# Cross attention of a decoder layer: seven block products for eight in the second element's queries and scores and in both elements' attended values

## The chip, the cores and the metric

The kernel runs on one core of a Trainium2 chip. A core has a matrix engine (TensorE, PE in the profile, whose weight loads are shown apart as PEld), three engines for elementwise work (VectorE or DVE, ScalarE or ACT, GpSimd or POOL), an engine that here only issues transfers (SyncE or SP), and 16 DMA engines. Each engine takes its instructions in the order written; semaphores make one wait for another. The on-chip memory SBUF has 128 partitions; TensorE writes to PSUM, a small memory of eight banks.

The metric is the time of one execution in microseconds (us), as the device measures it; lower is better. Several executions of the kernel before gave a median of 1125.8 us (1124.88 to 1126.19).

## The reference, cut to what matters

A decoder layer in float32 on x of shape (2, 512, 512): self attention with 16 heads, cross attention to a context of 1024 rows per element, a feed-forward part (FFN), each followed by a residual sum and a layernorm.

```python
x = layernorm(x + self_attention(x, ...))        # 16 heads of 128, weights as 4-bit codes times scales

Q = x @ W_qkv[:512].T                            # (2, 512, 512)
scores = coef * einsum('bsd,bnd->bsn', Q, ctx)   # (2, 512, 1024)
scores = scores - max(scores)
thr = top_k(scores, 54)[0][..., -1:]             # 54 are kept in each row
scores = where(scores < thr, -inf, scores)
x = layernorm(x + einsum('bsn,bnd->bsd', softmax(scores), ctx) @ W_o.T)

gate, up = split(x @ w_gate_up.T, 2)             # 2048 each
x = layernorm(x + (silu(gate) * up) @ w_down.T)
```

The cross attention is the part in question: a 512x512x512 product for the queries of each element, 512x512x1024 for the scores, 512x1024x512 for the attended values, and 512x512x512 for the projection behind them.

## The kernel before, in words

The 128 partitions hold the contracted dimension of every product. P is 128, KD = 4 pieces of 128 make the model dimension, NT = 4 tiles of 128 rows an element, NK = 8 pieces the 1024 context rows. HK = 2 and HS = HD = 256 are halves.

**Seven for eight.** `seven` (before, it serves the self attention's projections, `gu` of the FFN's first product and `pd` of its second) multiplies matrices cut into 2x2 blocks with seven block products in place of eight. It needs sums of blocks beforehand: four for the stationary side (`combine_a`) and four for the moving side (`combine_b`); `ALEFT` and `BRIGHT` map blocks and sums to the product numbers. One call makes two 128-row pieces of the output, 512 columns each, by products of 128x256. Products 1, 6 and 7 go to the bank `r`; after each, ScalarE keeps a copy in a buffer `u` (`keep`, L161 to L162). Products 2, 5, 4 and 3 go to the double bank `z`. VectorE then adds `z` and `u`: `on_second` for the second output half, `on_first` for the first. Product 3 is put off (`rest`) and issued inside the next call by `close`, so that TensorE does not wait for ScalarE.

**Cross attention.** It does not use `seven`. `xquery` (L346) makes Q with TensorE, 512 columns wide, and ScalarE copies each bank. `xscores` (L373) makes one tile of 128 rows by 1024 scores, which ScalarE evicts scaled by `coef` (L386). `clip` (L389) finds the 54th-largest score of each row on VectorE: MAX8 gives the eight largest, MATCH_REPLACE8 strikes them out, seven times; ScalarE then takes exponentials, VectorE masks and sums, and ScalarE scales. `xattend` (L448) multiplies the weights with the context and projects the result with `xpo` (L474), added to the residual. For element 0 the weights are transposed by TensorE (`transpose_weights`, L432); for element 1 `turn_weights` (L418) has VectorE transpose blocks of 32 and SP move them with 16 transfers a group (`turn`, L244). The queries' input x1T of element 1 and x2T of both are turned in the same way, which leaves rows in an order by blocks of 32; `in_order` and `turned` name the two orders.

**Order of the work.** It is written out by hand: engines run their parts in the order in which the program issues them, subject to a scheduler that moves independent instructions. The buffers are places in SBUF with a tag each (`place`), one tensor at a time; the tag decides when the next tensor may be written. Element 0's search runs beside the self attention; its attended values lie around `project(last)`, the last projection of the self attention (`ro` and `zo`). Then follow `xpo` of element 0, `xq` and `xs` of element 1, `up(0, 0)` and `down(0, 0)`, the first half of the FFN of element 0 (L861, L922), while element 1's search (`search1`) is advanced two steps with every block of `up`, then `up(0, 1)`, `xattend` of element 1, `down(0, 1)` and the FFN of element 1. In `up`, a block loads `wgu` (512 KB), GpSimd makes four sums (`wc`), and `seven` gives two results: VectorE's `ut` (L897) and `gt` (L903), which ScalarE turns into `sg` and VectorE multiplies into `h` (L906). Sums of `h`, `hc`, follow (L879 to L883). `combine_wdn` makes the second product's weight sums `dc` on GpSimd.

## Time and profile before

| | us |
|---|---|
| median of the runs | 1125.8 (1124.88 to 1126.19) |
| the profiled execution | 1123.9 |
| its span, first to last instruction | 1122.1 |
| TensorE busy | 1091.8 (97% of the span) |
| VectorE busy | 609.2 (54%) |
| GpSimd busy | 504.9 (45%) |
| ScalarE busy | 414.2 (37%) |
| xq of element 1, in the chain | 13.86 |
| xpo of element 0, in the chain | 13.73 |

An instruction line of the profile has the source line, engine, operation, output<-inputs by the program's names, the shape as partitions x elements, a count, busy time in us, mean ns of one, and behind the bar the engine's idle time just before, with what ended it. The chain of waits is followed back from the last instruction: at each piece to what released it, or to the one before on its engine. Matmuls overlap, and each float32 matmul has two records, so that the mean of one record is longer than the share of it that counts. The granted clock of TensorE was 0.998 of full speed.

### The profile page before, as it was taken

How to read it: one execution, taken by the hardware profiler on the slowest of the kernel's cores; microseconds unless marked ns; L12 is line 12 of the kernel's file. 1: busy time of each engine (PE TensorE's matmuls, PEld its weight loads, DVE VectorE, ACT ScalarE, POOL GpSimd, SP SyncE). 2: the span in 40 equal slices, each digit the busy share in tenths (PEclk: the TensorE clock that was granted, in tenths of full speed). 3: DMA queues.
4: the chain of work that ended last, by engine and by line, in shares of the span. 5: the costliest groups of instructions: out<-in, count | busy, mean ns of one | idle time of the engine just before them, and what ended most of it. 6: DMA issues, size and time to landing. Idle time of an engine off the chain costs nothing.

```text
span 1122.1 us, 12521 instructions
## 1 busy us (share of the span) xinstructions
PE 1091.8 (97%) x4144; PEld 775.2 (69%) x4144; DVE 609.2 (54%) x983; ACT 414.2 (37%) x927; POOL 504.9 (45%) x498
## 2 busy tenths in 40 slices
PE   7999999999999999999999999999999999999997
PEld 5666776677677667574657666446878886888886
DVE  5645445345444446278997543249995423543353
ACT  2453445335443534434445542123433212221221
POOL 4844725845945644523372430130445530464730
PEclk9999999999999999999999999999999999999999
DMA  9435545554554465433325446420214300520300
GB/s 353 125 101 173 171 122 205 181 174 136 181 191 110 135 219 163 144 100 107 103 92 181 112 109 232 129 56 19 95 38 161 121 20 19 169 85 29 133 18 37
DMA packets 66607, 141.63 MB, mean 126 GB/s; under 512 B 12656, under 2 KB 14704, under 8 KB 66544
## 3 DMA queue, kind: packets, MB, share of 16 engines
q1 hardware_dynamic: 66400, 140.32, 39.3%
q8 instruction: 33, 0.54, 0.2%
q10 hardware_dynamic: 144, 0.52, 0.1%
q14 instruction: 30, 0.25, 0.1%
HBM read 99.90 MB, written 2.10 MB: 91 GB/s over the span
## 4 chain that ended last, share of the span: by engine, by line
PE 74%; DVE 14%; ACT 5%; POOL 2%; DMA 2%; issue 1%; SPq 1%; DVEq 0%; ACTq 0%; POOLq 0%
PE sc L600 8%; PE av L643 8%; PE zqk L152 8%; PE zgu L152 6%; PE rqk L152 6%; PE xav L459 5%; PE rgu L152 5%; PE zo L152 4%; PE zv L152 4%; PE zpd L152 4%; DVE work L398 4%; PE ro L152 3%; DVE top L401 3%; PE rv L152 3%; PE rpd L152 3%; PE xq L351 2%
## 5 line engine op out<-in xcount | busy, mean ns | idle before, releaser
L643 PE MATMUL av<-pt,v 128*128 128x512 f32 x256 | 121.6, 592 | 0.0
L607 DVE TENSOR_REDUCE nm<-sc 128x2 f32<-128x1024 f32 x64 | 78.2, 1222 | 74.5 <-PE sc L600 74.5
L600 PE MATMUL sc<-k,q 128*128 128x512 f32 x256 | 117.3, 599 | 0.7 <-DVE q L586 0.5
L99 POOL TENSOR_TENSOR wc<-wqk 128x256 f32<-128x256 f32 x31 | 24.9, 803 | 191.6 <-PE zqk L152 179.2
L623 DVE STREAM_TRANSPOSE tq<-p 128x512 f32<-128x512 f32 x128 | 85.3, 699 | 34.8 <-ACT p L620 27.5
L620 ACT ACTIVATE p<-p,sm 128x512 f32<-128x512 f32 x128 | 86.2, 723 | 4.9 <-DVE sm L619 4.9
L600 PEld LDWEIGHTS sc<-k,q 128*128 128x128 f32 x256 | 47.3, 190 | 58.9 <-issue 51.2
L611 ACT ACTIVATE p<-sc,nm 128x512 f32<-128x512 f32 x128 | 86.9, 686 | 1.6 <-ACT nm L608 0.2
L522 POOL TENSOR_TENSOR wqk<-wqk,sqk 128x512 f32<-128x512 f32 x52 | 65.9, 1288 | 40.4 <-DMA wqk<-in_wqk 25.5
L162 ACT ACTIVATE ugu<-rgu 128x256 f32<-128x256 f32 x96 | 36.2, 378 | 101.8 <-PE rgu L152 101.8
L99 POOL TENSOR_TENSOR wc<-wgu 128x256 f32<-128x256 f32 x32 | 28.9, 902 | 95.0 <-PE zgu L152 67.0
L643 PEld LDWEIGHTS av<-pt,v 128*128 128x128 f32 x256 | 48.5, 190 | 31.0 <-issue 27.3
L162 ACT ACTIVATE uqk<-rqk,bqkv_sb 128x256 f32<-128x256 f32 x96 | 45.2, 474 | 66.5 <-PE rqk L152 65.3
L152 PE MATMUL rqk<-x0c,wc 128*128 128x256 f32 x256 | 67.3, 385 | 1.0 <-ACT uqk L162 0.6
L152 PE MATMUL rgu<-x2c,wc 128*128 128x256 f32 x256 | 66.2, 381 | 0.7 <-POOL wc L100 0.4
L152 PEld LDWEIGHTS rqk<-x0c,wc 128*128 128x128 f32 x256 | 46.9, 190 | 21.3 <-ACT uqk L162 10.7
L379 PE MATMUL xs<-memT,qt 128*128 128x512 f32 x128 | 57.9, 600 | 1.6 <-ACT p L611 1.3
L934 POOL TENSOR_TENSOR res<-res,upd 128x512 f32<-128x512 f32 x12 | 15.6, 1296 | 96.7 <-DVE res L933 96.7
L401 DVE MAX8 top<-work 128x8 f32<-128x1024 f32 x48 | 58.5, 1219 | 0.8
L459 PE MATMUL xav<-at,mem 128*128 128x256 f32 (+1 forms) x192 | 55.9, 450 | 0.0
L152 PEld LDWEIGHTS rgu<-x2c,wc 128*128 128x128 f32 x256 | 48.1, 190 | 8.9 <-POOL wc L100 1.6
L661 ACT ACTIVATE ot<-av,bqkv_sb 128x512 f32<-128x512 f32 x28 | 19.2, 687 | 85.9 <-PE av L643 85.9
(203 smaller groups left out, 2309.4 us busy)
## 6 DMA issues: line engine op xcount, KB each, us to landing
pt<-tq SPq DMA_DIRECT2D x512, 64.0 KB, 2.0
wgu<-in_wgu SPq DMA_DIRECT2D x32, 512.0 KB, 3.3
wqk<-in_wqk SPq DMA_DIRECT2D x28, 512.0 KB, 4.9
sqk<-in_wqk_s SPq DMA_DIRECT2D x27, 512.0 KB, 3.8
wdn<-in_wdn SPq DMA_DIRECT2D x4, 2048.0 KB, 8.3
wv<-in_wv SPq DMA_DIRECT2D x7, 1024.0 KB, 5.3
sv<-in_wv_s SPq DMA_DIRECT2D x14, 512.0 KB, 6.1
wo<-in_wo SPq DMA_DIRECT2D x7, 1024.0 KB, 5.3
```

Source lines behind the costliest of these rows:

```text
L152: nc.tensor.matmul(o, left[k][:, cols], right[k], start=start and k == 0, stop=k == len(left) - 1, skip_group_check=not start,)
L162: nc.scalar.activation(u[:, i, :], r, AF.Identity, bias=at)
L379: nc.tensor.matmul(sc[:, cols], qts[b][:, k, t * P : (t + 1) * P], memTs[b][k][:, cols], start=(k == 0), stop=(k == KD - 1),)
L401: nc.vector.max(top, work)
L459: nc.tensor.matmul(av[:, h * n : (h + 1) * n], mems[b][k][:, m * P : (m + 1) * P], ats[b][h][k], start=(k == 0), stop=(k == NK - 1),)
L522: eng.tensor_tensor(part[:, w], part[:, w], sct[:, w], ALU.mult)
L600: nc.tensor.matmul(scs[:, n, :], q[:, (t + n) * P : (t + n + 1) * P], k, start=True, stop=True,)
L607: nc.vector.reduce_max(nms, scs, axis=AX.X, negate=True)
L611: nc.scalar.activation(pr, scs[:, t % 2, :], AF.Exp, bias=nms[:, t % 2 : t % 2 + 1], scale=HSCALE, accum_out=sm,)
L620: nc.scalar.activation(pr, pr, AF.Copy, scale=sm)
L623: nc.vector.transpose(tq[:, :, :, t, :].rearrange("p n k c -> p k n c"), pr.rearrange("p (k n a) -> p k n a", n=NB, a=BLK),)
L643: nc.tensor.matmul(av, vs[u // GH][:, k, j * P : (j + 1) * P], pt[:, :, k, :], start=(k == 0), stop=(k == NT - 1),)
```

## The change

- `xquery` of element 1 is replaced by `seven_xquery`: `coef` is multiplied into wq by ScalarE, GpSimd makes the four sums of wq, `combine_turned` makes the sums of x1T on VectorE, and the results are added by VectorE (`put`) in place of ScalarE's copies. VectorE also makes the sums of the queries (`sums_a`) for the next step.
- `xscores` of element 1 is replaced by `seven_xscores`: four calls of `seven`, with sums of the context (`combine_memT`) made on GpSimd. A call gives two score tiles (s and 2 + s) half of their columns, added by VectorE. ScalarE's evictions go.
- `xattend` uses `seven` for both elements: sums of the context (`combine_mem`) on GpSimd, sums of the attention weights on VectorE (`combine_at` for element 0, inside `turn_weights` for element 1). The projection adds its four pieces in the order 0, 2, 3, 1.
- `seven` gets an option `late` that issues product 2 ahead of product 1.
- `combine_wdn(0, 0)` moves behind the scores. The second search takes the tiles in the order 0, 2, 1, 3 and has one work buffer in place of two. `up(0, ...)` has three buffers for `wgu` in place of four.

The queries and scores of element 0 stay as they are. The core of the diff:

```diff
+    def sums_a(eng, a, c, steps):
+        for n, w in enumerate(steps):
+            a00, a01, a10, a11 = (f[:, w] for f in a)
+            eng.tensor_tensor(c[0][n], a10, a11, ALU.add)
+            eng.tensor_tensor(c[1][n], c[0][n], a00, ALU.subtract)
+            yield
+            eng.tensor_tensor(a10, a00, a10, ALU.subtract)
+            eng.tensor_tensor(c[2][n], a01, c[1][n], ALU.subtract)
+            yield
+
+    def sums_b(eng, b, c):
+        b00, b01, b10, b11 = b
+        eng.tensor_tensor(c[0], b01, b00, ALU.subtract)
+        eng.tensor_tensor(c[1], b11, c[0], ALU.subtract)
+        eng.tensor_tensor(b01, b11, b01, ALU.subtract)
+        eng.tensor_tensor(c[2], b10, c[1], ALU.subtract)
+        return BRIGHT(b, (c[0], c[1], b01, c[2]))
...
+        if late:
+            product(2, z[:, 1, :])
         product(1, r)
         keep(0, bias[0])
-        product(2, z[:, 1, :])
+        if not late:
+            product(2, z[:, 1, :])
...
+    def put(dst, z, u, is_turned=True):
+        if not is_turned:
+            nc.vector.tensor_add(dst.rearrange("p (h s) -> p h s", h=2), z, u)
+            return
+        o = in_order(dst)
+        for h in range(2):
+            nc.vector.tensor_add(
+                o[:, 2 * h : 2 * h + 2],
+                *(f[:, h, :].rearrange("p (i t c) -> p i t c", t=NT, i=NB // 2) for f in (z, u)),
+            )
+
+    def seven_xquery(b, w_tag, q_tag, c_tags):
+        w = xw["wq"]
+        for k in range(KD):
+            nc.scalar.activation(w[:, k, :], w[:, k, :], AF.Copy, scale=coef)
+        wc = combine_a(nc.gpsimd, blocks_t(w), place(w_tag, (4, HK, HD), f"wqc{b}"))
+        qt = place(q_tag, (KD, S), f"qt{b}")
+        q4 = blocks_t(qt)
+        c12 = place(c_tags[0], (2, HK, HS), f"qc{b}_12")
+        c4 = place(c_tags[1], (HK, HS), f"qc{b}_4")
+        for m in range(HK):
+            def second(z, u, m=m):
+                put(qt[:, HK + m, :], z, u)
+            def first(z, u, m=m):
+                put(qt[:, m, :], z, u)
+                c = [c12[:, 0, m : m + 1]], [c12[:, 1, m : m + 1]], [c4[:, m : m + 1]]
+                for _ in sums_a(nc.vector, q4, c, [slice(m, m + 1)]):
+                    pass
+            seven(f"xq{b}_{m}", wc, xcs[b], slice(m * P, (m + 1) * P), second, first)
+        close()
+        qts[b] = ALEFT(q4, (c12[:, 0], c12[:, 1], q4[2], c4))
+
+    def combine_memT(b, tags):
+        mts = []
+        t4 = place(tags[2], (2, HK, HS), f"mT{b}_4")
+        for n in range(2):
+            g = slice(n * S, (n + 1) * S)
+            b4 = [f[:, :, g][:, :, h] for f in memTs[b] for h in (slice(0, HS), slice(HS, S))]
+            t12 = place(tags[n], (2, HK, HS), f"mT{b}_{n}")
+            mts.append(sums_b(nc.gpsimd, b4, (t12[:, 0], t12[:, 1], t4[:, n])))
+        memTs[b] = mts
+
+    def seven_xscores(b):
+        for s in range(NT // 2):
+            for n in range(2):
+                def add(z, u, s=s, n=n, h=1):
+                    o = sts[b, 2 * h + s][:, n * S : (n + 1) * S]
+                    put(o, z, u, False)
+                seven(
+                    f"xs{b}_{s}_{n}",
+                    qts[b],
+                    memTs[b][n],
+                    slice(s * P, (s + 1) * P),
+                    add,
+                    lambda z, u, add=add: add(z, u, h=0),
+                    late=s == 0 and n == 0,
+                )
+        close()
...
     def clips(b, tags):
-        for t in range(NT):
-            yield from clip(b, t, tags[t % len(tags)])
+        for n, t in enumerate(range(NT) if b == 0 else (0, 2, 1, 3)):
+            yield from clip(b, t, tags[n % len(tags)])
...
-        yield from turn([sts[b, t] for t in range(NT)], NK, list(shaped), dests)
+        b4, c = ats[b], []
+        for t, _ in enumerate(turn([sts[b, t] for t in range(NT)], NK, list(shaped), dests)):
+            yield
+            if t == 1:
+                two = place(c_tags[0], (2, NK // 2, NT * 2, BLK), f"atc{b}")
+                c = [two[:, 0], two[:, 1], place(c_tags[1], (NK // 2, NT * 2, BLK), f"atc{b}_4")]
+            for g in (0, 1) if t == 1 else (t,) if t > 1 else ():
+                sums_b(nc.vector, *([f[:, :, g::NT, :] for f in fs] for fs in (b4, c)))
+        ats[b] = BRIGHT(b4, (c[0], c[1], b4[1], c[2]))
...
+    def combine_mem(b, tags):
+        hk = NK // 2
+        a4 = [f[:, :, h] for f in mems[b] for h in (slice(0, HD), slice(HD, D))]
+        a4 = a4[0], a4[2], a4[1], a4[3]
...
+        steps = [slice(k, k + 2) for k in range(0, hk, 2)]
+        mems[b] = ALEFT(a4, (c1, c2, a4[2], [c[:, k] for c in c4 for k in range(hk // 2)]))
+        yield from sums_a(
+            nc.gpsimd, a4, ([c1[:, w] for w in steps], [c2[:, w] for w in steps], c4), steps
+        )
+
+    def combine_at(b, tags):
+        c = [place(tag, (NK // 2, HS), f"atc{b}_{n}") for n, tag in enumerate(tags)]
+        ats[b] = sums_b(nc.vector, ats[b], c)
...
     def xattend(b, ot_tags):
+        oth = [place(tag, (2, S), f"xo{b}_{n}") for n, tag in enumerate(ot_tags)]
+        ot = [t[:, n, :] for t in oth for n in range(2)]
+        for m in range(HK):
+            seven(
+                f"xav{b}_{m}",
+                mems[b],
+                ats[b],
+                slice(m * P, (m + 1) * P),
+                lambda z, u, m=m: put(ot[HK + m], z, u, b == 1),
+                lambda z, u, m=m: put(ot[m], z, u, b == 1),
+            )
             yield
+        close()
         for t in range(NT):
             po = bank("r", f"xpo{b}_{t}")
-            for k in range(KD):
+            for k in (0, 2, 3, 1):
...
+            free_sc = [f"sc{(scale_count[0] + n) % 3}" for n in range(3)]
+            for _ in combine_mem(0, ("wqk2", *free_sc[:2])):
+                pass
             transpose_weights(0, ("xT1", "xc1"))
     load_memT(1)
+    combine_at(0, (free_sc[2], "work", "ot0"))
...
     turn_x(1, "v0", "v1", "x1T")
+    combine_turned(nc.vector, 1, "v0", "x1")
...
+    combine_memT(1, ("wqk3", "wqk4", "ot1"))
...
-            wt = place(("sc0", "sc1", "wqk1", "wqk2")[n % 4], (KD, 2, P), f"wgu{i}_{b}")
+            wt = place(("sc0", "sc1", "wqk1", "wqk2")[n % (3 + b)], (KD, 2, P), f"wgu{i}_{b}")
...
     load_wdn(0, 0)
-    for _ in combine_wdn(0, 0):
-        pass
     layernorm(0, "b")
     turn_x(0, "xc0", "xT0", "x2T")
     combine_turned(nc.vector, 0, "xc0", "x2")
-    xquery(1)
+    seven_xquery(1, "xT1", "xc1", ("sc1", "p3"))
     score_tiles(1, (("v0", 2), ("v1", 2)))
-    for t in range(NT):
-        xscores(1, t)
-    search1 = clips(1, ("sc2", "work"))
-    hc = up(0, 0, nc.vector, search1)
+    seven_xscores(1)
+    for _ in combine_wdn(0, 0):
+        pass
+    search1 = clips(1, ("work",))
+    hc = up(0, 0, nc.vector, search1, combine_mem(1, ("wqk2", "sc2", "p2", "p3")))
     down(0, 0, hc)
     load_wdn(0, 1)
-    search1 = chain(search1, turn_weights(1, ("ot0", "ot1", "ot0", "ot1"), ("cmb0", "cmb1")))
+    search1 = chain(search1, turn_weights(1, ("ot0", "ot1", "ot0", "ot1"), ("cmb0", "cmb1"), ("v0", "work")))
```

## The prediction, made before the changed kernel ran

> **What bounds the kernel now.** I read the page's busy times and slices first, then the chain of waits, the groups and stretches of the middle of the kernel, and last the timeline of TensorE where it idles.
>
> ```profile
> span 1122.1 us, 12521 instructions
> PE 1091.8 (97%) x4144; PEld 775.2 (69%) x4144; DVE 609.2 (54%) x983; ACT 414.2 (37%) x927; POOL 504.9 (45%) x498
> PE   7999999999999999999999999999999999999997
> DVE  5645445345444446278997543249995423543353
> PE 74%; DVE 14%; ACT 5%; POOL 2%; DMA 2%; issue 1%; SPq 1%; DVEq 0%; ACTq 0%; POOLq 0%
> ```
>
> TensorE is busy in 97% of the span at full granted clock, and is 74% of the chain. So products taken from it shorten the kernel, unless somebody else is late there. VectorE's slices show the two places where that can be: two runs of 9s, the searches for the 54th-largest score; the later one lies from 757 to 841 us. The chain shows the stages to be changed:
>
> ```profile
> 698.09 18.88 PE xav L459 x44
> 716.97 13.73 PE xpo L474 x32
> 730.70 13.86 PE xq L351 x32
> 744.57 7.93 PE xs L379 x18
> 753.24 1.24 DVE top L392
> 797.61 0.68 DVE ut L897
> ```
>
> From 698 to 752 TensorE works without a break. From 753 the chain runs over VectorE's search, and between 797 and 830 it runs on VectorE almost throughout. What the engines do there, by stretch (from and to, then busy us and count of PE, PEld, DVE, ACT, POOL, then clock, DMA share, GB/s):
>
> ```profile
> 700.00:720.00 20.00, 20.00 (x48) 8.93 (x47) 4.18 (x11) 4.87 (x8) 0.00 (x0) 1.00 0.42 119
> 740.00:760.00 20.00, 20.00 (x47) 8.57 (x46) 9.18 (x14) 3.67 (x6) 0.00 (x0) 1.00 0.19 46
> 760.00:780.00 20.00, 19.75 (x61) 11.14 (x60) 19.66 (x26) 7.90 (x12) 0.00 (x0) 1.00 0.08 27
> 800.00:820.00 20.00, 20.00 (x94) 17.39 (x93) 19.97 (x33) 5.47 (x13) 8.16 (x10) 1.00 0.24 79
> 820.00:840.00 20.00, 18.40 (x83) 15.14 (x82) 19.83 (x31) 7.94 (x11) 10.15 (x12) 1.00 0.08 27
> ```
>
> Before 760 VectorE and GpSimd have room. From 760 to 840 VectorE is full, and TensorE loses its first microseconds to it:
>
> ```profile
> 830.51 0.70 PE L152 MATMUL zpd<-wdn,h 128*128 128x256 f32 x2 [0.78 <-DVE h L906]
> 864.49 1.10 PE L152 MATMUL zgu<-x2T,wc 128*128 128x256 f32 x4 [1.31 <-DVE ut L897]
> ```
>
> **What is removed.** The products' price comes from these groups (each matmul has two records) and the chain:
>
> ```profile
> L351 PE MATMUL xq<-x1T,wq 128*128 128x512 f32 x64 | 28.1, 594 | 0.0
> L459 PE MATMUL xav<-at,mem 128*128 128x512 f32 x64 | 28.0, 592 | 0.0
> L459 PE MATMUL xav<-at,mem 128*128 128x256 f32 x128 | 28.0, 379 | 0.0
> L379 PE MATMUL xs<-memT,qt 128*128 128x512 f32 x128 | 57.9, 600 | 1.6 <-ACT p L611 1.3 <-ACT s L386 0.3
> ```
>
> The xpo piece of the chain has 32 records in 13.73 us, 0.429 us each; a 128x256 record takes half, and eight of them 1.73 us. So xq of the second element is 13.7 us, xs of it 27.5 us, xav of each element 27.5 us. One eighth of each goes: 1.72 + 3.44 + 3.44 + 3.44 = **12.0 us**. That is the ceiling: nothing else leaves TensorE.
>
> **What is added, stage by stage.**
>
> *Sums of mem for element 0* (8 GpSimd additions of 128x512, 1.27 us each by the oc and vc groups, 10.2 us) are queued before the last wo blocks' dequantisation. GpSimd is busy 9.43 of 20 us from 620 to 640 and 7.43 from 640 to 660; the last output block needs its combined weights over 25 us later. I take 0. Without that cover each late microsecond would be one of TensorE's, 10.2 at most.
>
> *Sums of the attention weights of element 0* (4 VectorE operations of 128x1024, about 1.2 us each by the MAX8 row of that width) follow the eight ScalarE copies. TensorE still has about 5 us of other products and the first two of xattend, which need no sum. 0; up to 3 if GpSimd's sums of memT meet VectorE's operations.
>
> *project(last), layernorm, the way to x1T.* The attended products of element 0 leave less filler, so the last projection ends about 4.7 us later (702.6 for 697.9). The 16 transfers of x1T, now issued from 705.5 to 714.9 with 2.0 us to landing, then land by 722; the four new sums of x1T (0.69 us each, as the x2 ones) are done by 725. TensorE wants x1T at 727.1 (730.7 less 3.44) and its sums two products, 1.7 us, later. 0, with 4 to 5 us to spare.
>
> *Sums of memT (8), of mem (8, two of them left for the search) and of wq (4)* for element 1 are 18 GpSimd additions here, 22.9 us. GpSimd is empty from 680 to 720, and the wq sums, queued last, wait for xT1, which xattend(0) frees; they end near 720 against 727. 0.
> The wdn sums, moved behind the scores, then fill 720 to 736. The first wgu load of up(0,0) that has to wait for qc1's buffer gets it near 761, is combined by 768 and wanted at 770.7: 0, but tight.
>
> *xq to xs.* Before, ScalarE copies of qt followed each bank. Now the last product must be kept, added by two put operations and summed by three of the 128x256 additions on VectorE (0.41 us each where alone) ahead of the products of xs that use sums; "late" puts another product first to cover part. I take **0.5 us**, between 0 and 1.5.
>
> *xs to the search.* This is where the gain is given back. TensorE reaches up(0,0) 8.6 us earlier (1.72 + 3.44 + 3.44), but a score tile is complete only after its second half's seventh product and two additions: I place the first MAX8 at 756.2, 3 us later than now. From there, by the changed kernel's order of instructions, VectorE has to do 17 MAX8 and 15 MATCH_REPLACE8 before the last h of this half (1.25 to 1.275 us with their loads: 40.8), two s operations 2.6, one transpose 1.2, 24 operations ut, gt and h at 0.61 start to start (14.6), sums of h 4.4, four puts 2.5, small ones 0.6: 66.7 us. The same pricing on the 23 and 19 of the kernel before, with its share of the rest, gives 78.5, where the trace has 77.2 (753.24 to 830.46). So the last h comes at 821.8 to 823 instead of 830.5, while TensorE wants it at 819.7. TensorE's idle time in this half goes from 1.85 to about 3.1: **+1.3 us**.
>
> *The rest of the search* moves into down(0,0) and the first blocks of up(0,1). ut of the third such block is done about 41 us after that h, and TensorE wants it at 38.3. With one work buffer, each tile's exponentials on ScalarE keep VectorE waiting up to 1 us before the next tile. I expect 3.4 us of idle time in place of 1.31 + 0.41: **+1.7 us**.
>
> *Attention weights of element 1*: 16 additions of 128x256 on VectorE between the turning transfers. The last transfer lands near 886 (SP issues them in order, among wgu loads), its sums end at 888, TensorE wants them at 890.5. 0, and 2 us to spare. xpo's order of k hides the last two puts. ScalarE gets lighter, because eviction of 16 score banks (0.69 us each) becomes three keeps of 128x256 per seven. The second half of the FFN of element 0 from the second down on, and all of element 1's, is as before. For the tight hand-overs together (sums of at, wgu, turned weights) I add **0.5 us**.
>
> [...] The row first: an addition of h (hc, L882) takes 0.41 us alone and 0.95 beside GpSimd's 1.70 us one, so a meeting costs about 0.5 us on VectorE and as much on GpSimd. Of the 28 added GpSimd operations few meet two-input VectorE work, since VectorE is busy only 13.4 of the 40 us after 680; six meetings would be 3 us, off the path.
> [...]
>
> **The sum.** -12.0 + 0.5 + 1.3 + 1.7 + 0.5 = -8.0 us. The profiled execution took 1123.9 (span 1122.1, 1.8 around it), 1.9 below the median 1125.8 of the runs. It would become 1115.9 (span 1114.1), the median **1117.8**.
>
> **Rivals.**
> 1. *VectorE absorbs it.* If the search starts with the second half's add at about 753 as now, and transfers keep their room, only 0 to 1.5 us come back: 1113.8 to 1115.3. For it: the pricing above came out 1.3 us too long on the kernel before.
> 2. *VectorE becomes the bound* from the first score to the third block of up(0,1). If the put operations and sums collide with GpSimd and the last h moves only to 827 to 829, the extra stall there is 5 to 7 us instead of 1.3, and with 1.7 more later 1121 to 1123.5. For it: VectorE is at 19.8 of 20 us for 80 us. Against it: six MAX8 and four MATCH_REPLACE8 fewer stand before that h.
> 3. *Slower: the gate weights with three buffers for four.* A buffer is freed by its unit's last product and wanted combined two units later, 2 x 14 x 0.432 = 12.1 us. Load (3.3) and four sums (0.73 each, 2.9) need 6.2. If SP's order (16 turning transfers are 10 us of issue) makes every load over 6 us late, each unit waits; the gain is gone from 1.0 us a unit in eight units, and from 1.3 (10.3 us in all) the kernel is slower. At 1.5: -8 + 12 = +4, 1129.8. Against it: only the turning stretches put such a queue on SP.
> 4. *The change doesn't do what it says*: if the seven products ran at more than 1.73 us per eight records, no gain. The gu products have this form already, at 385 ns against 379 for xav.
>
> **How the numbers follow.** My forecast's own case (1115.3 to 1120.5) has 0.55, rival 1 0.13, rival 2 0.20; 0.06 lies between it and no gain, rival 3 has 0.06. Differences under 0.2% (2.3 us) can't be told from no change here. Faster than 1123.5 are the first three, 0.88; same 0.06, slower 0.06. The range 1114.0 to 1123.0 leaves out about 0.16.
>
> **What would show it.** Right: xav, xq and xs as 128x256 products, 24.1, 12.0 and 24.1 us for an element; xq starting near 727, up(0,0) near 763; first MAX8 of the second search near 756; VectorE full until about 862; TensorE's idle time ahead of zpd and zgu ended by VectorE's h and ut, 3 to 4 us more in all; GpSimd busy near 540. Wrong: idle time of TensorE ended by GpSimd's wc or by wgu's transfers in every unit, by x1T before xq, or by the turned weights before xav of the second element.

## The result, and the profile after

The changed kernel took 1119.8 us (median of seven executions, 1117.0 to 1122.7), the kernel before 1125.2 beside it: ratio 0.9948, 95% interval 0.9932 to 0.9965. Run again on another chip it had 0.9954 (0.9939 to 0.9969). It is faster by half a per cent, 5 to 6 us where 8.0 were forecast; the forecast range, 1114.0 to 1123.0, holds it.

The page of the profiled execution (1119.8 us) has these lines in place of those of before: span, busy times, the slices of TensorE and VectorE, and the chain of waits by engine.

```profile
span 1118.0 us, 12865 instructions
PE 1083.0 (97%) x4248; PEld 798.0 (71%) x4248; DVE 641.1 (57%) x1043; ACT 415.3 (37%) x941; POOL 540.3 (48%) x526
PE   7999999999999999999999999989999899999997
DVE  5544445435345436268997554468999733543353
PE 72%; DVE 15%; ACT 6%; DMA 2%; POOL 2%; issue 1%; DVEq 0%; ACTq 0%; POOLq 0%; SPq 0%
```

TensorE's row has 8s now where it had only 9s: in the slices from 727 to 755 and from 866 to 894 us. The matmul groups say that the change does what it says. Of xq, xav and xs, 64 + 64 + 128 records of 128x512 fell to 32 + 0 + 64, and 128 records of 128x256 (xav) to none. Counted in units of 128x256 that is 448 fewer, and 392 new ones came. 56 x 0.216 = 12.1 us of products are gone. What came in their place is in TensorE's timeline (start, us, instruction, then the idle time before it and what ended it):

```profile
714.07 2.00 PE L174 MATMUL rxav<-at,mem 128*128 128x256 f32 x8 [0.48 <-ACT uxav L184]
716.54 1.13 PE L590 MATMUL xpo<-wo,xo 128*128 128x512 f32 x2 [0.47 <-ACT uxav L184]
737.73 1.13 PE L174 MATMUL rxq<-x1c,wqc 128*128 128x256 f32 x4 [0.95 <-ACT uxq L184]
746.63 1.13 PE L174 MATMUL zxq<-x1T,wqc 128*128 128x256 f32 x4 [2.15 <-DVE qt L396]
749.56 0.70 PE L174 MATMUL zxs<-mT,qc 128*128 128x256 f32 x2 [0.26 <-DVE qc L134]
823.41 0.70 PE L174 MATMUL zpd<-wdn,h 128*128 128x256 f32 x2 [0.43 <-DVE h L1028]
871.12 1.13 PE L174 MATMUL zgu<-x2T,wc 128*128 128x256 f32 x4 [3.09 <-DVE ut L1019]
```

With 0.45 and 0.38 near 660 and 672, 0.20 and 0.23, TensorE's idle time in the changed part is 9.1 us; the same list of before adds up to 3.85. So 5.2 of the 12.1 us went to new waits. Another 1.0 was lost before the change begins: a product that started at 633.78 starts at 634.74, and from 35 to 40 us this execution has a granted clock of 0.66 where the profile before has 1.00 (the last section comes back to it). That leaves 1.8 to the measured 4.1 of the spans. Between that product and the zpd product near 960 us TensorE's busy time fell by 10.5 us, not by 12.1. Each restart costs a little (the first four records after a wait take 1.10 to 1.13 us, not 1.03), but there are only four waits more than before, some 0.4 us by an estimate of 0.1 each; the rest I can't place.

Two waits are the big ones: 2.15 at the hand-over from queries to scores, 3.09 in the second half of the FFN of element 0. VectorE's timeline ahead of the first shows its queue at work, not idle:

```profile
742.28 1.03 DVE L134 TENSOR_TENSOR qc<-qt 128x256 f32<-128x256 f32 x1
743.35 0.83 DVE L135 TENSOR_TENSOR qc<-qc,qt 128x256 f32<-128x256 f32 x1
744.11 0.94 DVE L137 TENSOR_TENSOR qt<-qt 128x256 f32<-128x256 f32 x1
744.97 0.94 DVE L138 TENSOR_TENSOR qc<-qt,qc 128x256 f32<-128x256 f32 x1
745.83 0.74 DVE L396 TENSOR_TENSOR qt<-zxq,uxq 128x256 f32<-128x256 f32 x2
```

The put that TensorE waits for is the last line. Ahead of it in VectorE's queue are the four sums of the first piece, at 0.83 to 1.03 us where 0.42 is the time alone (in the run without the down weights' sums, below). On GpSimd the sums of the down weights, which were to be done by 736, last until 743, and the gate weights' sums queued behind them fill the microseconds of the queries' sums:

```profile
733.17 1.26 POOL L976 TENSOR_TENSOR dc<-wdn 128x512 f32<-128x512 f32 x1 [11.01 <-DVE mvb L321]
741.77 1.27 POOL L980 TENSOR_TENSOR dc<-wdn,dc 128x512 f32<-128x512 f32 x1
742.99 0.91 POOL L99 TENSOR_TENSOR wc<-wgu 128x256 f32<-128x256 f32 x1
745.59 0.90 POOL L99 TENSOR_TENSOR wc<-wgu 128x256 f32<-128x256 f32 x1
```

The down weights' sums began at 725.3 before, at 733.2 now. SP issues the load of wdn at 724.64 instead of 717.00, with 8.4 us to landing. (VectorE is named as the releaser at 733, but the load landed at that moment.) The load does not wait for its place, which holds the context of element 0: the last product that reads this context ends at 716.1. It stands in SP's queue behind the 16 transfers of x1T. SP's timeline before:

```profile
705.49 10.01 SPq L257 DMA_DIRECT2D x1T<-x1Tt  x16
717.00 0.37 SPq L840 DMA_DIRECT2D wdn<-in_wdn  x1
```

and after:

```profile
714.52 10.02 SPq L282 DMA_DIRECT2D x1T<-x1Tt  x16
724.64 0.53 SPq L962 DMA_DIRECT2D wdn<-in_wdn  x1
```

x1T's transfers start 9.0 us later. 6.3 of that is the last projection, whose last output product starts at 703.40 instead of 697.06. The other 2.7 are on ScalarE: the first scaling of wq by `coef`, new with the change, stands in its queue ahead of the normalisation from which x1T is made, and waits for the load of wq:

```profile
710.21 0.72 ACT L405 ACTIVATE wq<-wq,coef 128x512 f32<-128x512 f32 x1 [2.42 <-DMA wq<-in_xwq]
710.84 2.91 ACT L329 ACTIVATE res<-res,nba,sda 128x512 f32<-128x512 f32 x4
```

From that last product to x1T's first transfer it is 8.4 us in the kernel before and 8.5 in the run with the attended values alone, which do not scale wq, and 11.1 in the changed kernel and in the run with queries and scores alone, which do. No run moves the scaling by itself.

### The profile page after: what moved, and what is told of

It reads as the page before. It is cut to its first block, busy times and chain, and to the rows that moved or that the text cites. A ratio compares the mean times of both kernels' runs of the same rounds, so it can differ in the third digit from the quotient of the medians.

```text
span 1118.0 us, 12865 instructions
## 1 busy us (share of the span) xinstructions
PE 1083.0 (97%) x4248; PEld 798.0 (71%) x4248; DVE 641.1 (57%) x1043; ACT 415.3 (37%) x941; POOL 540.3 (48%) x526
## 4 chain that ended last, share of the span: by engine, by line
PE 72%; DVE 15%; ACT 6%; DMA 2%; POOL 2%; issue 1%; DVEq 0%; ACTq 0%; POOLq 0%; SPq 0%
PE av L759 8%; PE sc L716 8%; PE zqk L174 8%; PE rqk L174 6%; PE zgu L174 6%; PE rgu L174 4%; PE zo L174 4%; PE zv L174 4%; PE zpd L174 4%; PE ro L174 3%; PE rv L174 3%; DVE work L490 3%; PE rpd L174 3%; DVE top L493 3%; PE xpo L590 2%; PE zxav L174 2%
## 5 line engine op out<-in xcount | busy, mean ns | idle before, releaser
L490 DVE MATCH_REPLACE8 work<-top,work 128x1024 f32<-128x1024 f32 x40 | 48.3, 1209 | 0.0
L702 DVE TENSOR_TENSOR q<-zqk,uqk 128x512 f32<-128x512 f32 x32 | 22.0, 687 | 42.2 <-PE zqk L174 42.1
```

The costliest lines, as they stand in the source:

```text
L490: nc.vector.match_replace(work, top, src, LOWEST)
```

## The experiments

**Is the late start of the search the cause of the 3.09?** The first MAX8 came at 763.5, not at 756.2. Tile 2 is complete earlier than tile 0.

```diff
-        for n, t in enumerate(range(NT) if b == 0 else (0, 2, 1, 3)):
+        for n, t in enumerate(range(NT) if b == 0 else (2, 0, 3, 1)):
...
+        order = (2, 3, 0, 1)
...
-        for t, _ in enumerate(turn([sts[b, t] for t in range(NT)], NK, list(shaped), dests)):
+        for t, _ in enumerate(turn(tiles, NK, list(shaped), dests, order)):
```

> Only the order of the second search changes: the tiles 2, 0, 3, 1 in place of 0, 2, 1, 3, and the turning follows. In the changed kernel the score tile 2 is complete at 759.3 us (third addition, 758.57 + 0.69), tile 0 only at 763.5 (fourth), where the first MAX8 starts. Theory A (TensorE's 3.09 us of idle time before the third block of up(0,1) is the late start of the search, carried along on VectorE): the first MAX8 comes at about 759.3, the 3.09 goes to 0.5 or less, the 0.43 and 0.20 before go too, span about 1114.5. Rival B (that idle time comes from the search's waits for ScalarE's exponentials with one work buffer, or from sums of the turned weights): 2 us or more of it stays, gain below 1 us.

1123.85 us (1122.7 to 1125.7), ratio 0.999 (0.9979 to 1.0): nearly all of the change's gain lost. The MAX8 came at 757.6, 6 us earlier, and the 0.43 and 0.20 between 800 and 825 went; but TensorE's timeline has

```profile
770.15 1.13 PE L174 MATMUL zxs<-memT,qc 128*128 128x256 f32 x4 [0.43 <-DVE s L392]
862.48 1.10 PE L174 MATMUL zgu<-x2T,wc 128*128 128x256 f32 x4 [2.37 <-DVE ut L1021]
900.29 1.22 PE L174 MATMUL zgu<-x2T,wc 128*128 128x256 f32 x4 [2.43 <-DVE ut L1021]
```

(The sums of the turned weights change their place with the order, from v0 to v1.) Theory A fell: with an earlier search the waits come at other blocks and are not shorter in sum.

**Is it VectorE's amount of work?** One round fewer in each tile of the search:

```diff
-        for r in range((CLIP_K - 1) // 8):
+        for r in range((CLIP_K - 1) // 8 - b):
```

> One round fewer (a MATCH_REPLACE8 and a MAX8) in each tile of the second search, so that its threshold is the 46th-largest score: the result is wrong, VectorE has 4 x 2.5 = 10 us less work between 763 and 865. Theory A (VectorE's backlog is what TensorE waits for there): the idle times 0.20, 0.43, 3.09 and 0.23 go, 3.5 to 4 us, span about 1114. Rival B (they come from elsewhere, such as late transfers or ScalarE's order): gain below 1 us.

1125.0 us, ratio 0.9996 (0.9984 to 1.0008): with 10 us less work on the busy engine the kernel is 4 to 5 us slower than the changed one. The waits of 0.20 and 0.43 went; in their place came 2.28 (ended by gt) at 865.67, 1.20 (ut) at 886.08 and 2.26 (a transfer of wgu) at 889.45. VectorE's timeline ahead of the first:

```profile
860.71 1.48 DVE L145 TENSOR_TENSOR atc<-at,atc 128x256 f32<-128x256 f32 x1
862.12 1.49 DVE L146 TENSOR_TENSOR at<-at 128x256 f32<-128x256 f32 x1
863.53 1.48 DVE L147 TENSOR_TENSOR atc<-at,atc 128x256 f32<-128x256 f32 x1
864.93 0.68 DVE L1025 TENSOR_TENSOR gt<-zgu,ugu 128x512 f32<-128x512 f32 x1
```

The sums of the turned weights, 0.41 us alone, take 1.48 each, and gt stands behind three of them. GpSimd runs the second half's down-weight sums, 1.44 to 1.77 us each, at that time. So neither the start of the search nor its length is the cause, and both theories of mine for the 3.09 fell (most of what both runs lost, 3.4 of 4 to 5 us by an estimate, is lower clock behind their new waits, see the last section). A third, C: VectorE and GpSimd get in each other's way.

**Theory C for the 3.09.** Keep GpSimd's down-weight sums from running there, by a place that comes free late:

```diff
-            tag = ("cmb", "tq")[b + half > 0]
+            tag = ("cmb", "tq")[b > 0]
...
-    hc = up(0, 1, nc.vector, search1, combine_wdn(0, 1))
+    hc = up(0, 1, nc.vector, search1)
...
     for _ in xattend(1, ("ot0", "ot1")):
         pass
+    for _ in combine_wdn(0, 1):
+        pass
```

> The GpSimd sums of the second half's down weights of element 0 (8 additions, 10 us at 852 to 863 in the changed kernel) are put in the places of the turned weights of element 1 and so can't begin before its attended values are done (about 921); they are wanted at about 941. Theory C (the 3.09 us of idle time before the third block of up(0,1) is VectorE slowed by GpSimd: between 860 and 871 its operations with two SBUF inputs took 1.58, 1.75, 0.93, 0.87 and 1.21 us where 0.68, 1.27, 0.41, 0.41 and 0.68 are the times alone, 2.9 us more): they take their times alone, the 3.09 goes to 0.8 or less and the stretch of half TensorE clock behind it, where there is one, goes with it; 2.5 to 4 us off the changed kernel's median of 1119.8. Rival B (VectorE's order, with sums and transposes ahead of ut, costs this at any speed): 2 us or more of the idle time stays, gain below 1 us.

1117.4 us (1115.6 to 1118.5), ratio 0.9933 (0.9914 to 0.9951). The 3.09 is 0.85. VectorE's groups between 860.0 and 871.2 in the changed kernel (busy us, mean ns behind the first bar):

```profile
L1028 DVE TENSOR_TENSOR h<-ut,sg 128x512 f32<-128x512 f32 x2 | 2.8, 1396 | 0.0
L499 DVE SCALAR_TENSOR_TENSOR s<-s,top,work 128x1024 f32<-128x1024 f32 x1 | 1.7, 1748 | 0.0
L146 DVE TENSOR_TENSOR at<-at 128x256 f32<-128x256 f32 x1 | 0.9, 932 | 0.0
L1019 DVE TENSOR_TENSOR ut<-zgu,ugu 128x512 f32<-128x512 f32 x1 | 0.7, 678 | 0.0
```

and between 855 and 872 here:

```profile
L1028 DVE TENSOR_TENSOR h<-ut,sg 128x512 f32<-128x512 f32 x2 | 1.4, 679 | 0.0
L499 DVE SCALAR_TENSOR_TENSOR s<-s,top,work 128x1024 f32<-128x1024 f32 x1 | 1.3, 1272 | 0.0
L146 DVE TENSOR_TENSOR at<-at 128x256 f32<-128x256 f32 x1 | 0.4, 414 | 0.0
L1019 DVE TENSOR_TENSOR ut<-zgu,ugu 128x512 f32<-128x512 f32 x2 | 1.3, 674 | 0.0
```

Same order, same operations; those with two operands in SBUF lose their excess (2 x 0.72 + 0.48 + 0.52, and 0.47 on L147: 2.9 us), and ut, which reads PSUM, has none to lose (678 and 674 ns). Theory C holds for 2.2 of the 3.09. The 0.85 that stays I put down to VectorE's backlog; no run takes it apart.

**The 2.15 at the hand-over: the queue, or the neighbour?** First the queue: one set of sums for both pieces, behind the last put.

```diff
-                c = [c12[:, 0, m : m + 1]], [c12[:, 1, m : m + 1]], [c4[:, m : m + 1]]
-                for _ in sums_a(nc.vector, q4, c, [slice(m, m + 1)]):
-                    pass
+                if m == HK - 1:
+                    for _ in sums_a(nc.vector, q4, ([c12[:, 0]], [c12[:, 1]], [c4]), [slice(0, HK)]):
+                        pass
```

> The sums of the queries are made once for both 128-row pieces (four additions of 128x512 after the last put) and so don't stand between the first and the second piece's put operations on VectorE. Theory A (TensorE's 2.15 us of idle time at 744.5 to 746.6 is product 3 of the second piece waiting for a put that is queued behind four sums): the 2.15 goes, and the first score product that uses a sum waits 1 to 2 us instead, net gain 0 to 1.2 us. Rival B (the wait is for ScalarE's keep or the products' own order): 1.5 us or more of the idle time before that product stays.

The 2.15 and 0.26 went, 0.42 came in their place, and the 0.95 became 1.33: the queue is where the wait is. The median was 1119.6 (ratio 0.995, 0.9934 to 0.9967), no better than the changed kernel: behind the unchanged 3.09 this profiled execution has a stretch of half clock (0.66 over 870 to 875 us, last section), which the changed kernel's does not (1.00).

Then the neighbour, by leaving out the down-weight sums of the first half:

```diff
+        if b + half == 0:
+            c = [a00, a01, a10, a11]
...
-        for k in range(0, NQ, 2):
+        for k in range(0, NQ if b + half else 0, 2):
```

> The eight GpSimd sums of the first half's down weights of element 0 are left out (raw blocks stand in for them, so the FFN's result is wrong). GpSimd is then free earlier and its sums of the first gate weights, too, end before the queries' sums. Theory A (the queries' sums on VectorE take 0.83 to 1.03 us instead of 0.42 because GpSimd works beside them): they take 0.41 to 0.45, the 2.15 us of idle time falls to 0.3 or less, span about 2 us shorter. Rival B (the four sums are in the way at any speed): they get short, but 1 us or more of the idle time stays.

The sums take 0.42 each and both waits are gone; even the 0.95 is 0.33. At any order of the queue, then, four sums of 0.42 are no hindrance. In the 0.95, too, GpSimd was the neighbour: VectorE's small operation ahead of ScalarE's normalisation (nbb, two operands in SBUF) takes 0.16 us here and 0.79 in the changed kernel, and the difference is about the 0.62 that the wait lost. The total (1121.5, ratio 0.9968, 0.9957 to 0.9978) did not follow, since new waits came later, two of them on GpSimd's gate-weight sums:

```profile
862.59 1.13 PE L174 MATMUL zgu<-x2c,wc 128*128 128x256 f32 x4 [0.95 <-POOL wc L99]
871.15 1.98 PE L174 MATMUL zgu<-x2c,wc 128*128 128x256 f32 x4 [1.66 <-POOL wc L99]
876.31 1.13 PE L174 MATMUL zgu<-x2T,wc 128*128 128x256 f32 x4 [1.42 <-DVE ut L1022]
```

GpSimd there mixes the second half's down-weight sums into the gate weights' (0.90 to 2.25 us each): the static order of its queue had shifted.

The same with nothing left out: these sums in places that the queries' products use until 747.

```diff
-            tag = ("cmb", "tq")[b + half > 0]
-            two = place(f"{tag}{n}", (2, NQ, HD), f"dc{b}_{half}_{n}")
+            tag = f"tq{n}" if b + half else ("xT1", "xc1")[n]
+            two = place(tag, (2, NQ, HD), f"dc{b}_{half}_{n}")
...
-        for tag in (("xT1", "xc1"), ("cmb0", "cmb1"))[b]:
+        for tag in (("xT1", "xc1"), ("cmb0", "cmb1"))[b or not half]:
```

> The GpSimd sums of the first half's down weights of element 0 change places with the sums of h, so that they wait for the sums of wq to be used up (747) and lie after the queries' sums, not beside them. Theory (GpSimd's neighbourhood makes the queries' sums slow, as the run without these sums said): the four sums take 0.41 to 0.45 us each, the 2.15 us of idle time goes to 0.3 or less, 1.5 to 2.5 us off the changed kernel's time; the 3.09 us later stays. Rival: the sums move into the search and cost there what they save here, no gain.

The first piece's sums, those ahead of the put, and the put in this kernel's timeline:

```profile
742.38 0.43 DVE L134 TENSOR_TENSOR qc<-qt 128x256 f32<-128x256 f32 x1
743.52 0.42 DVE L138 TENSOR_TENSOR qc<-qt,qc 128x256 f32<-128x256 f32 x1
743.86 0.75 DVE L396 TENSOR_TENSOR qt<-zxq,uxq 128x256 f32<-128x256 f32 x2
```

The put comes 2 us earlier and the wait is gone. The second piece's sums still meet GpSimd (0.80 to 1.49), and nobody waits for them that long. 1119.1 us, ratio 0.9941 (0.992 to 0.9961): 3.08 remains before the third block, with a stretch of half clock behind it (0.73 over 870 to 875 us, last section).

**What is each half of the change worth?** Only the attended values (the calls of `seven_xquery` and `seven_xscores` put back):

```diff
-    seven_xquery(1, "xT1", "xc1", ("sc1", "p3"))
+    xquery(1)
...
-    seven_xscores(1)
+    for t in range(NT):
+        xscores(1, t)
```

> Only the attended values of both elements use seven products; queries and scores of element 1 are as before (the single work buffer, the order 0, 2, 1, 3 and three buffers for the gate weights stay as changed). TensorE loses 6.88 us of products. If the losses lie where the trace of the changed kernel has them, this part adds 0.45 + 0.38 + 0.48 + 0.47 us of idle time around element 0, none at the hand-over from queries to scores, and its share of the 3.09: 1120 to 1121 against 1125.9 before, about as good as the whole change. If the two parts are worth what they take off TensorE: 6.9/12.0 of the gain, 1122.3.

1120.0 us, ratio 0.9958 (0.9943 to 0.9973), as expected; but the 0.48 and 0.47 near 715 are not there. The same four normalising operations stand ahead of ScalarE's keep, but they start at 706.51 and not at 710.84, with no scaling of wq ahead of them. Only queries and scores (`xattend`, `transpose_weights`, `turn_weights`, `load_mem` put back as they were):

```diff
-    combine_at(0, (free_sc[2], "work", "ot0"))
...
-    hc = up(0, 0, nc.vector, search1, combine_mem(1, ("wqk2", "sc2", "p2", "p3")))
+    hc = up(0, 0, nc.vector, search1)
```

> Only queries and scores of element 1 use seven products; attended values as before. TensorE loses 5.16 us of products, and gets 2.15 + 0.26 + about 0.9 us of idle time at the hand-over, and the late start of the search. If the losses lie where the trace of the changed kernel has them: 1123 to 1125, a gain of 1 to 2.5 us. If the parts are worth what they take off TensorE: 5.2/12.0 of the gain, 1123.4 (both agree here; the trace tells by the idle times).

1119.3 us, ratio 0.9943 (0.9921 to 0.9964). Each half gives as much as the whole. The second beat both expectations, and its profile says why: its load of wdn is issued at 719.73, GpSimd's sums of it end at 738, the queries' sums take 0.42, the 2.15 is absent; and without sums of turned weights the wait before the third block is 0.25, with the search starting as late as 762.7. Together they meet what neither meets alone: the load of wdn is issued at 720.32 in the first, 719.73 in the second and 724.64 with both. The first half by itself has 0.72, 2.28 and 2.12 us of waits on VectorE at 820, 864 and 897, where its 128x256 sums take up to 1.21 us on average.

**Both moves together, and ScalarE's keeps.** The last large waits are 0.48, 0.47 and 0.95 (0.33 once the first half's sums are moved), ended by ScalarE's keeps; ahead of them in its queue are four normalising operations.

```diff
+        if (b, name) in ((1, "a"), (0, "b")):
+            for t in range(NT):
+                r = res[b, t]
+                nc.vector.tensor_scalar(r, r, mv[:, t, 0:1], sd[:, t : t + 1], ALU.subtract, ALU.mult)
+            return
```

> Both moves of down-weight sums together. If the two idle times have separate causes, as the single runs said (2.15 and 0.26 gone by the one, 2.2 of 3.09 by the other), the gains add: 4 to 5 us of TensorE's idle time less than in the changed kernel, about 1115 to 1115.5. Rival: VectorE reaches the third block with the same backlog, because what the earlier search gains is taken by sums that moved beside it; then no better than the second move alone, 1117.4.

> Both moves, and the normalisation of element 1 ahead of x1T and of element 0 ahead of x2T is done by VectorE (four operations of 128x512 with two per-row numbers, 0.61 us each as at the end of the kernel) in place of ScalarE's four of 0.73. Theory (TensorE's 0.48, 0.47 and 0.95 to 1.3 us ended by ScalarE's keeps are keeps queued behind those four): these three go, 1.5 to 2 us more off than with both moves alone, 1113 to 1114. Rival (the keeps wait for TensorE's own products, or VectorE's queue becomes as late): less than 0.7 us.

> The changed kernel itself, on the same chip and beside the same runs of the kernel before: 1117 to 1122.7 as in its first runs, ratio 0.994 to 0.996; executions without a stretch of half TensorE clock besides the one at the end near 1117.5, with one 1119.5 to 1120.5.

| kernel | us | ratio to before |
|---|---|---|
| before | 1126.2 (1123.6 to 1126.8) | |
| the change, again | 1120.7 (1117.1 to 1122.3) | 0.9954 (0.9939 to 0.9969) |
| both moves | 1114.1 (1114.0 to 1114.9) | 0.9899 (0.9884 to 0.9913) |
| both moves, normalising on VectorE | 1113.4 (1112.1 to 1114.0) | 0.9888 (0.9875 to 0.9901) |

Both moves bring 6 us more, a little more than expected: the gains add, and at the medians the ceiling of 12.1 us is reached. TensorE's waits in the changed part add up to 4.0 us with both moves, as before the change (3.85). Between the two profiles, though, the way from the product at 634 us to zpd near 960 is 10.3 us shorter; what the medians differ by beyond that lies outside the changed part, and no run explains it. From 735 to 870 the last kernel's TensorE waits only for

```profile
805.48 1.13 PE L174 MATMUL zgu<-x2T,wgu 128*128 128x256 f32 x4 [0.20 <-DVE gt L1030]
820.78 0.70 PE L174 MATMUL zpd<-wdn,h 128*128 128x256 f32 x2 [0.44 <-DVE h L1033]
865.90 1.13 PE L174 MATMUL zgu<-x2T,wc 128*128 128x256 f32 x4 [0.85 <-DVE ut L1024]
```

The keep at the queries went as expected, but those at the attended values turned into 0.86 (still a keep) and 0.32 (a put). There the normalisation was not what held them up: in ScalarE's queue the scaling of wq still stands ahead of the keep and waits 2.42 us for its load. The third step is worth 0.7 us at the medians, with intervals that overlap. The 1120.7 and the spread of the repeated run confirm the first result. Its expectation that executions near 1117.5 have no extra stretch of half clock is not borne out: the profiled execution, 1117.1 us, has one (0.71 over 745 to 750 us, last section).

**The order of the search again, with the collisions gone.**

> Both moves, the normalisation on VectorE, and the second search in the order 2, 0, 3, 1. What remains of idle time that VectorE ends between 800 and 870 is 0.20 + 0.44 + 0.85 = 1.5 us. Theory (the order was bad before only because the earlier search pushed VectorE's sums of turned weights beside GpSimd's sums of down weights, which now lie elsewhere): the three go and nothing comes in their place, 1112 against 1113.4. Rival (it brings the sums of turned weights and the gate units out of step by itself): idle times of 2 us or more near 860 and 900 come back, 1115 or more.

1117.4 us (1116.4 to 1121.1), ratio 0.9928 (0.9912 to 0.9943): 4 us worse. VectorE stands still in front of a sum whose transfer has not landed, with gt and ut queued behind, and TensorE waits at 881 (1.24) and 897 (2.65). The profiled execution is the slowest of the five, 1121.1 us:

```profile
879.34 0.58 DVE L144 TENSOR_TENSOR atc<-at,at 128x256 f32<-128x256 f32 x1 [4.34 <-DMA at<-att]
888.72 0.42 DVE L144 TENSOR_TENSOR atc<-at,at 128x256 f32<-128x256 f32 x1 [2.84 <-DMA at<-att]
```

SP issues the 64 turning transfers one by one from 837 to 887, about 0.62 us each, between the loads of wgu. An order that starts the search earlier writes the sums into VectorE's queue ahead of data that SP cannot deliver sooner. The rival is right: this order hurts also with the collisions gone.

## Why the prediction was right, and where it was not

- *The ceiling, -12.0 us*: right (56 units, 12.1). So was the direction, and the price of seven products.
- *Sums of mem, x1T's way, three buffers for the gate weights, the turned weights*: right at 0. In the changed kernel TensorE never waits for x1T, for a transfer of wgu or for at. Rival 3 did not occur. For x1T the 0 is in part luck: its sums ended at 732.3 and not by 725, since the projection ended later than taken and the scaling of wq, which has no term in the sum, held up the normalisation; TensorE itself came to xq at 730.6 instead of 727.1.
- *xq to xs, +0.5 (0 to 1.5)*: wrong, and the term that failed most: 0.95 + 2.15 + 0.26 = 3.4 us, 2.9 more than taken and beyond its bound. The step that failed is "the wdn sums then fill 720 to 736": the load behind them moved from 717.0 to 724.6, so they ran from 733 to 743, and the gate sums behind them until 749, beside the queries' sums. It could not hold by the prediction's own numbers: x1T's 16 transfers, moved by the 4.7 us of the last projection, are issued until 719.6, and the load of wdn stands behind them in SP's queue. The prediction priced the queries' sums at 0.41 "where alone" and did not ask who was alone.
- *GpSimd beside VectorE, "six meetings would be 3 us, off the path"*: about the right size for a place it did not look at, and on the path: 2.9 us between 860 and 871, 2 us between 742 and 746. The run without the sums and the two moves show it. Its row was misread: the addition of 0.95 (at 828.04) lies beside sums of 0.97 and 0.79; the one of 1.70 had ended at 826.6. The first half of rival 2, sums that collide with GpSimd, came true; its second, a last h at 827 to 829, did not.
- *xs to the search, +1.3*: wrong, it was -1.2 (0.20 + 0.43 us of idle time in place of 1.85). The first MAX8 came at 763.5, not 756.2. But the last h came at 822.3 to 823.4, 60 us later and not 66.7 (16 MAX8 and 14 MATCH_REPLACE8 went ahead of it, not 17 and 15), and TensorE, expected there at 819.7, arrived at 823.0, so that the wait before zpd was 0.43 (0.78 and 0.23 before). The profile before had VectorE full there, and I took that as a price.
- *The rest of the search, +1.7*: right in size (3.09 + 0.23 for 1.72), wrong in cause. It was put down to VectorE's backlog; the move of the second down-weight sums shows that 2.2 of 3.09 were GpSimd's neighbourhood, and with 10 us less of the search other waits took its place.
- *Tight hand-overs, +0.5*: 0.45 + 0.38 - 0.28 + 0.48 + 0.47 = 1.5. "ScalarE gets lighter" was true in sum (0.69 us evictions gone), but it is the order of its queue that counts: at 711 the scaling of wq, waiting for its load, and four normalising operations stand ahead of the keeps, at 735 four normalising operations. The keep at the queries went when these left ScalarE. Those at the attended values did not, and were absent in the run that normalises on ScalarE but does not scale wq; that the scaling makes these waits rests on this comparison.
- *The sum*: +0.5, +1.3, +1.7 and +0.5 make 4.0; measured were +3.4, -1.2, +1.6 and +1.5, 5.2 in all. That the time fell into the range is in part luck, because a term 2.5 too high stood against two that were 2.9 and 1.0 too low. Outside these terms another 2.8 us went, 1.0 ahead of the change and the 1.8 that I can't place; TensorE came to up(0,0) at 770.4 and not near 763.

## What to carry to other kernels

When a change takes work from the bounding engine and hands sums to two others, price the sums by who will be running beside them after the change, and follow each load through the queue that issues it: here one load stood behind 16 transfers, came 7.6 us later with them and moved GpSimd's sums beside VectorE's. Part of that delay was a small new operation, the scaling of wq, that waited for its own load ahead of work that was ready. Busy shares do not show this (VectorE 57% after the change, 54% before); the duration of one form, against its shortest, does (0.83 to 1.03 us against 0.42). A static order of in-order queues makes "less work" no promise: both an earlier start and a shorter search were slower (1123.9 and 1125.0 us against 1119.8). Moving GpSimd's sums to where nobody waits for VectorE's two-operand work doubled the gain of the change (from 5.5 to 12.1 us beside the same runs).

## What the runs showed of the hardware

*Two-operand work in SBUF.* Beside GpSimd, VectorE's additions of 128x256 went from 0.41 to as much as 1.03 (changed kernel) and at worst 1.49 us (short search), h from 0.68 to 1.21 and 1.58, the two-operand scalar_tensor_tensor of 128x1024 from 1.27 to 1.75, that of 128x4 from 0.16 to 0.79; GpSimd's own went from 0.73 to 0.9 to 1.7 and from 1.27 to as much as 2.25. ut, gt and the scores' puts, which read one operand from PSUM (0.65 to 0.69), and MAX8 and MATCH_REPLACE8 (1.19 to 1.23) stayed the same. Over the nine operations taken apart above (five between 860 and 871 us, 2.9 us, and the four sums from 742 to 746, 2.1 us) the excess is 0.55 us a meeting on average, beside GpSimd instructions of 0.80 to 1.73. What it is that the two engines hold each other up at, no run shows.

*A wait on TensorE can cost more than its length.* After some waits the granted clock falls to half (0.50) for a few microseconds. The repeated run of the changed kernel, in TensorE's timeline:

```profile
743.82 1.49 PE L174 MATMUL zxq<-x1T,wqc 128*128 128x256 f32 x4 [2.16 <-DVE qt L396]
```

and its view by stretches from 745 to 750 (from and to, length, then busy us and count of PE, PEld, DVE, ACT, POOL, then clock, DMA share, GB/s):

```profile
745.00:750.00 5.00, 5.00 (x18) 4.12 (x18) 2.41 (x6) 0.68 (x2) 1.42 (x3) 0.71 0.12 29
```

From 740 to 745 the clock is 0.95, from 750 to 755 it is 1.00. Microsecond by microsecond such a stretch can be read in the changed kernel's first profile, behind a wait of 1.91 us that ends at 35.67: 0.70 from 36, 0.50 from 37 and from 38, 0.59 from 39 and 1.00 from 40. In the run with the first move alone, the timeline and then the stretch behind its 3.08:

```profile
869.14 1.97 PE L174 MATMUL zgu<-x2T,wc 128*128 128x256 f32 x4 [3.08 <-DVE ut L1019]
```

Its view by stretches, in the same columns:

```profile
870.00:875.00 5.00, 5.00 (x18) 4.13 (x17) 3.86 (x7) 1.40 (x3) 3.35 (x4) 0.73 0.20 53
```

18 records in five microseconds, where the next five have 25 at a clock of 1.00. With 0.93 of the clock in the 5 us before, 5 x (0.07 + 0.27) = 1.7 us of products are lost by an estimate from these clocks, on top of the 3.08 of waiting. The profiled execution of the changed kernel had the same two waits (2.15, 3.09) with the clock at 1.00 throughout behind them; why the one execution has the stretch and the other not, no run shows. Over the profiles of this study, one execution of each kernel and two of the changed one, 9 of the 16 waits of 2.1 to 3.1 us in the changed part were followed by such a stretch, and so was one of 1.66 (the run without down-weight sums, at 871, clock 0.66 from 870 to 875); of the waits of 0.75 to 1.42 us none was by itself. The order run had two (behind 2.37 and 2.43), the short search two (behind 2.28 and 2.26), which at the estimated 1.7 us each is 3.4 of the 4 to 5 us that they lost. In both moves together no wait in the changed part is over 0.9, and its four executions lie within 0.9 us of one another, those of the changed kernel within 5.7. That the spread comes from these stretches is consistent with the granted clocks of its executions (three with 0.999 at 1117.0 to 1117.9, four with 0.996 to 0.997 at 1119.8 to 1122.7), and not shown. There is such a place ahead of anything changed, too: the kernel before and the changed one each wait 1.91 us for a keep near 35 us, and behind it the clock over 35 to 40 us is 1.00 in the one and 0.66 in the other. Over 20 to 40 us, 10 of the 14 profiles, the changed kernel's first among them, have 0.91 to 0.93; those of the kernel before, of the changed kernel's repeated run, of the first order run and of the attended values alone have 1.00. The kernel before spreads as well, from 1123.1 to 1127.5 us in the 25 executions beside the first experiments. And the stretches don't explain every difference: each of the two profiles of the changed kernel has one, at 35 us in the execution of 1119.8 and at 745 in that of 1117.1.
